# Paged attention on one core: projections of two token tiles by seven block products, with stored weight sums and head columns passed through DRAM

## The chip, the core and the metric

The kernel runs on one core of one Trainium2 chip. The metric is the device time of one launch in microseconds (us). The kernel before took 2164.35 us, the median of three runs between 2163.95 and 2166.38. Its profile is one further execution with a span of 2166.3 us.

Engine names are those of the profile: PE is the matmul engine (PEld its weight loads), DVE the vector engine, ACT the scalar engine, POOL GpSimd, and SP the engine whose queue issues most DMA transfers.

## The reference

There are 64 sequences of 32 tokens with 512 channels. All arithmetic is in fp32.

```
x = x + einsum('bct,bcd->bdt', x, weights[condition])      # a 32x32 mix of tokens per sequence
q, k, v = x Wq^T, x Wk^T, x Wv^T                           # 32, 8 and 8 heads of 128
q, k = rope(rmsnorm(q) * q_norm_w), rope(rmsnorm(k) * k_norm_w)
keys, values = 512 cached positions by page table, then the 32 new ones
x = x + softmax(q keys^T / sqrt(128), masked by cache length) values Wo^T
```

Four query heads share one key head. The page table of a sequence names 16 pages of 32 positions.

## The kernel before

Tokens are packed into 16 tiles of 128 rows, four sequences to a tile. The heads are worked in two halves of 16 query heads and 4 key heads, so there are 32 **steps**: 16 tiles for half 0 and then the same tiles for half 1. Half 0 keeps the transposed input and the running output of a tile in DRAM (`x1t_d`, `acc_d`) and half 1 loads them again.

A step has 16 **slots**: four sequences (batches) by four key heads. In each slot PE does the `scores` of one head (four 128x128 products) and, one slot later, its `values` (four 128x129 products). Into these slots the loop at L949 lays other work by a table (`pieces`, L888): while step n runs its attention, step n+1 gets its projections. `k_a` stands at slot 3, the four `q_a` at slots 4 to 7 and `v_a` at slot 13; each is four 128x512 products (`project`, L420). The output projection of step n-1 stands at slots 8 and 9 with eight 128x512 products each (`out_proj`). At slot 0 `new_scores` (L606) reads all the head columns of the step, and at slots 1 and 3 `new_values` follows.

A projected group goes through `norm_rope` (L428): a square on ACT, a power on POOL and about seven operations on DVE. `turn_rows` then transposes 32x32 blocks into the SBUF tile `rows`, and `spread` (L482) copies them by DMA, sixteen transfers a step, to the tiles `q_cols` and `q_last` in which heads lie as columns. `spread` of three batches stands at slot 9, that of batch 2 at slot 11, since `q_cols` of a batch is free only when its scores have been done.

Cached keys come by `load_k` (L292): sixteen page transfers of 64 KB for each batch, issued by SP two batches ahead, into two buffers. `head_keys` (L582) copies one head of them on DVE into one of four `kh` buffers, four slots before the scores read it. Cached values are gathered by POOL, one 256 KB chunk a slot, and masked by ACT.

PE and SP work in the order in which the program is written (`manual_schedule`). On DVE, ACT and POOL a scheduler set the order when the kernel was built. An engine that meets a wait holds everything behind it. The SP queue is therefore one line for key pages, spreads, inputs and stores. A last part of the code (`exact`) repeats the whole computation with masks and is entered only where a denominator leaves its range.

Of the kernel before, what the change touches and what calls it, by code (L numbers as in the profile page):

```python
# [19 lines left out]
P = 128  # L20
# [28 lines left out]
RAW = 3  # L49
WARM = 10  # L50
# [5 lines left out]
def cond_resid_paged_attention_kernel(  # L56
# [52 lines left out]
    bd = const.tile([P, P], F32, tag="bd", name="bd")  # L109
    nc.vector.memset(bd, 0.0)  # L110
# [8 lines left out]
    cos = const.tile([P, NT, HD], F32, tag="cos", name="cos")  # L119
    sin = const.tile([P, NT, HD], F32, tag="sin", name="sin")  # L120
# [10 lines left out]

    def angles(t0, tmp):

        reduced(t0, tmp)
        sines(t0, tmp)
# [19 lines left out]
    def sines(t0, tmp):  # L155
        t1 = t0 + TRIG
        _, turns, red = (tmp[:, i, :] for i in range(3))
        nc.scalar.activation(sin[:, t0:t1, :].rearrange("p t f -> p (t f)"), red, AF.Sin)
        nc.scalar.activation(turns, red, AF.Abs)
        nc.scalar.activation(  # L160
            cos[:, t0:t1, :].rearrange("p t f -> p (t f)"),
            turns,
            AF.Sin,
            bias=half_pi,
            scale=-1.0,
        )
# [21 lines left out]
    acc_d = [dram.tile([P, HID], F32, tag=f"acc_d{t}", name=f"acc_d{t}") for t in range(NT)]  # L188

# [5 lines left out]
    def steps_of(exact, pools):  # L195
# [34 lines left out]
        rows = wpool.tile([P, 4, GH + 1, P], F32, tag="rows", name=f"rows_{uid}")  # L230
# [48 lines left out]
        def load_cond_weights(t, eng=nc.sync, kind=mybir.EngineType.SP):  # L279
            number = conditions(t, kind)  # L280
            for i in range(BT):
                blk = slice(i * S, (i + 1) * S)
                eng.dma_start(
                    bd[blk, blk],
# [69 lines left out]
        class Step:  # L354
            def __init__(self, n):
                self.n, self.hh, self.t = n, n // NT, n % NT
                self.name = f"{n}_{uid}"

        def x1_a(st):

            st.acc = work.tile([P, HID], F32, tag="acc", name=f"acc_{st.name}", bufs=3)
# [9 lines left out]
        def x1_c(st):  # L371
# [3 lines left out]
            nc.tensor.matmul(pm, bd, st.acc, start=True, stop=True)  # L375
            nc.vector.tensor_tensor(st.acc, pm, st.acc, ALU.add)

        def x1_b(st):
# [5 lines left out]
            st.x1t = work.tile([P, KC, P], F32, tag="x1t", name=f"x1t_{st.name}", bufs=1)  # L384
# [7 lines left out]
        def rot_tables(st):  # L392

            st.rot = {}
            c, s = cos[:, st.t, :], sin[:, st.t, :]
            for name, w in norm_w.items():
                cw = work.tile(
                    [P, 2, HD],
                    F32,
                    tag=f"cw_{name}",  # L400
                    name=f"cw_{name}_{st.name}",
                    bufs=1,
                )
                sw = work.tile(
                    [P, 2, HD],
                    F32,
                    tag=f"sw_{name}",
                    name=f"sw_{name}_{st.name}",
                    bufs=1,
                )  # L410
                w1, w2 = w[:, 0:HD], w[:, HD:D]
                nc.gpsimd.tensor_tensor(cw[:, 0, :], w1, c, ALU.mult)
                nc.gpsimd.tensor_tensor(cw[:, 1, :], w2, c, ALU.mult)
                nc.vector.scalar_tensor_tensor(
                    sw[:, 0, :], w2, -1.0, s, ALU.mult, ALU.mult
                )
                nc.gpsimd.tensor_tensor(sw[:, 1, :], w1, s, ALU.mult)
                st.rot[name] = cw, sw
# [9 lines left out]
        def norm_rope(st, pp, name, kind, to=None):  # L428

            cw, sw = st.rot[kind]  # L430
# [39 lines left out]
        def turn_rows(st, i, rd, name):  # L470


            nc.vector.transpose(
                rows[:, :, i, :].rearrange("p k (h s) -> p h k s", h=4),
                rd.rearrange("p h (k d) -> p h k d", k=4),
            )

        def columns(st, bt):

            return q_last[st.n % 2] if bt == BT - 1 else q_cols[:, bt]  # L480

        def spread(st, batches):  # L482


            for bt in batches:
                for k in range(4):
                    nc.sync.dma_start(
                        columns(st, bt)[k * S : (k + 1) * S, :, :],
                        rows[bt * S : (bt + 1) * S, k, :, :],
                    )  # L490
# [3 lines left out]

# [610 lines left out]
```

## Time and profile before

| What | Value |
|---|---|
| Median of three runs | 2164.35 us |
| Profiled execution, span | 2166.3 us |
| PE busy | 2144.2 us, 99% of the span |
| DVE busy | 1196.5 us, 55% |
| ACT busy | 868.9 us, 40% |
| POOL busy | 804.7 us, 37% |
| 128x512 products in q, k and v projections | 768, shown as 1536 instructions |
| DMA moved | 357.51 MB, mean 165 GB/s |
| SP transfers of key pages | 2048, 64 KB each |
| SP transfers of head columns | 480, 80 KB each |

An fp32 product is two matmul instructions in the profile, so a projection of four products is a line with x8. Matmuls overlap, so a product is priced by the distance from start to start, and not by its busy time. A DMA that SP issues is shown with the time that SP needs for the issue; the transfer itself goes on after it.

### The profile page before, as it was taken

What the parts mean: (1) busy time and instruction counts of PE and PEld (TensorE: products, weight loads), DVE (VectorE), ACT (ScalarE), POOL (GpSimd) and SP (SyncE); (2) the same over time, 40 slices, a digit from 0 to 9 for tenths busy, and PEclk for the clock granted to TensorE, in tenths of its full rate; (3) what the DMA queues carried; (4) which work ended last, traced back from release to release, by engine and by line L of the source; (5) the groups of instructions that cost most, each with busy time, mean ns of one, the idle gap of its engine ahead of it and who ended that gap; (6) DMA issues with size and microseconds to landing.
All of it is one profiled execution on the core that took longest, in us unless ns stands there. A gap on an engine that the chain in (4) does not pass through costs nothing.

```text
span 2166.3 us, 41552 instructions
## 1 busy us (share of the span) xinstructions
PE 2144.2 (99%) x12972; PEld 1494.4 (69%) x12972; DVE 1196.5 (55%) x2883; ACT 868.9 (40%) x1577; POOL 804.7 (37%) x1005
## 2 busy tenths in 40 slices
PE   7999999999999999999999999999999999999998
PEld 4766777667776677766777766777666777667775
DVE  5666555666455564465554565644566545556442
ACT  3544444444333344333444333443334443334441
POOL 4433333433333343333433343433434333334330
PEclk9999999999999999999999999999999999999999
DMA  8765555555655556556766855565545565555551
GB/s 248 193 164 162 157 172 157 148 155 160 172 152 152 151 160 174 154 150 196 224 177 179 212 158 164 157 178 159 156 141 169 162 174 159 153 153 163 171 162 54
DMA packets 387638, 357.51 MB, mean 165 GB/s; under 512 B 55024, under 2 KB 317296, under 8 KB 387408
## 3 DMA queue, kind: packets, MB, share of 16 engines
q1 hardware_dynamic: 342864, 213.87, 35.1%
q0 software_dynamic: 41648, 136.74, 21.6%
q10 hardware_dynamic: 2896, 4.14, 0.5%
q8 instruction: 106, 1.74, 0.3%
q14 instruction: 124, 1.02, 0.2%
HBM read 302.64 MB, written 12.58 MB: 146 GB/s over the span
## 4 chain that ended last, share of the span: by engine, by line
PE 97%; ACT 0%; issue 0%; DVE 0%
PE po_x L653 22%; PE ps_x L595 21%; PE pout_x L541 20%; PE pp_q_x L423 20%; PE pp_k_x L423 5%; PE pp_v_x L423 5%; PE pnv_x L637 2%; PE psn_x L613 1%; PE pmix_x L375 1%; PE px1t_x L383 0%; PE pt_x L467 0%; ACT pr_x L603 0%; ACT v_x L346 0%; DVE acc_x L549 0%; ACT nv_x L645 0%
## 5 line engine op out<-in xcount | busy, mean ns | idle before, releaser
L333 POOL DMA_INDIRECT raw_x<-in_vc_dram,v_row x512 | 540.4, 1055 | 820.4 <-ACT v_x L346 752.0
L603 ACT ACTIVATE pr_x<-ps_x 128x512 f32<-128x512 f32 x512 | 305.9, 597 | 825.5 <-PE ps_x L595 756.8
L653 PEld LDWEIGHTS po_x<-v_x,pr_x 128*128 128x128 f32 x4096 | 515.7, 192 | 126.9 <-issue 114.5
L653 PE MATMUL po_x<-v_x,pr_x 128*128 128x129 f32 x4096 | 551.1, 277 | 2.3 <-ACT pr_x L603 1.6
L423 PE MATMUL pp_q_x<-wq_x,x1t_x 128*128 128x512 f32 x1024 | 463.2, 595 | 8.5 <-ACT x1t_x L385 8.2
L541 PE MATMUL pout_x<-wo_x,ot_x 128*128 128x512 f32 x1024 | 450.2, 592 | 0.0
L595 PE MATMUL ps_x<-q_cols_x,kh_x 128*128 128x128 f32 x3072 | 405.4, 275 | 0.0
L595 PEld LDWEIGHTS ps_x<-q_cols_x,kh_x 128*128 128x128 f32 x3072 | 376.1, 192 | 15.1 <-issue 14.6
L346 ACT ACTIVATE v_x<-raw_x,valid 128x512 f32<-128x512 f32 x512 | 363.0, 716 | 5.3 <-DMA raw_x<-in_vc_dram,v_row 5.1
L541 PEld LDWEIGHTS pout_x<-wo_x,ot_x 128*128 128x128 f32 x1024 | 189.7, 190 | 214.3 <-issue 214.0
L423 PEld LDWEIGHTS pp_q_x<-wq_x,x1t_x 128*128 128x128 f32 x1024 | 185.8, 191 | 194.4 <-issue 185.6
L588 DVE COPY kh_x<-k_t_x 128x512 f32<-128x512 f32 x506 | 206.0, 417 | 188.1 <-PE ps_x L595 153.8
L671 DVE TENSOR_TENSOR nv_x<-po_x,nv_x 128x258 f32<-128x258 f32 x256 | 108.4, 424 | 314.9 <-PE po_x L653 279.9
L440 POOL TENSOR_TENSOR rs_q_x<-ms_q_x,minus_half 128x4 f32<-128x4 f32 x128 | 140.8, 1100 | 170.1 <-DVE ms_q_x L438 169.9
L433 ACT ACTIVATE sq_q_x<-pp_q_x 128x512 f32<-128x512 f32 x128 | 76.6, 598 | 272.9 <-PE pp_q_x L423 178.9
L595 PE MATMUL ps_x<-q_last_x,kh_x 128*128 128x128 f32 x1024 | 135.2, 275 | 0.0
L549 DVE TENSOR_TENSOR acc_x<-pout_x,acc_x 128x512 f32<-128x512 f32 x32 | 22.1, 692 | 199.3 <-PE pout_x L541 199.3
L595 PEld LDWEIGHTS ps_x<-q_last_x,kh_x 128*128 128x128 f32 x1024 | 124.6, 192 | 0.0
L423 PE MATMUL pp_k_x<-wk_x,x1t_x 128*128 128x512 f32 x256 | 116.3, 597 | 0.9 <-ACT x1t_x L385 0.9
L423 PE MATMUL pp_v_x<-wv_x,x1t_x 128*128 128x512 f32 x256 | 115.2, 592 | 0.0
L674 DVE TENSOR_TENSOR o_x<-nv_x,rden 128x256 f32<-128x256 f32 x256 | 108.6, 424 | 6.2
L437 DVE TENSOR_REDUCE ms_q_x<-sq_q_x 128x4 f32<-128x512 f32 x128 | 86.5, 676 | 45.1 <-ACT sq_q_x L433 44.6
(105 smaller groups left out, 1455.1 us busy)
## 6 DMA issues: line engine op xcount, KB each, us to landing
k_t_x<-in_kt_dram SPq DMA_DIRECT2D x2048, 64.0 KB
q_cols_x<-rows_x SPq DMA_DIRECT2D x360, 80.0 KB
q_last_x<-rows_x SPq DMA_DIRECT2D x120, 80.0 KB
raw_x<-in_vc_dram,v_row POOLq DMA_INDIRECT x512
wo_x<-in_wo_dram SPq DMA_DIRECT2D x32, 256.0 KB
acc_x<-in_x_dram SPq DMA_DIRECT2D x16, 256.0 KB
acc_d<-acc_x SPq DMA_DIRECT2D x16, 256.0 KB
wq_x<-in_wq_dram SPq DMA_DIRECT2D x8, 512.0 KB
```

The lines of the kernel that those rows point to most:

```text
L333: nc.gpsimd.indirect_dma_start(out=raw.rearrange("p g d -> p (g d)"), out_offset=None, in_=vc, in_offset=bass.IndirectOffsetOnAxis(ap=v_ro ...
L346: nc.scalar.activation(v_bufs[b % 2][:, c, :, 0:D], raw, AF.Copy, scale=ok)
L423: nc.tensor.matmul(pp, st.x1t[:, c, :], w[:, c, :], start=(c == 0), stop=(c == KC - 1))
L437: nc.vector.tensor_reduce(ms, sq, AX.X, ALU.add)
L440: nc.gpsimd.tensor_tensor(rs, ms, minus_half, ALU.pow)
L541: nc.tensor.matmul(st.po, st.ot[:, i, :], wt["o", st.hh, i // 4][:, i % 4, :], start=(i == 0), stop=(i == QH - 1),)
L588: last["dve"] = nc.vector.tensor_copy(k, ba.k_raw[:, :, g, :]).ins
L595: nc.tensor.matmul(ps[:, c, :], ba.k[g][:, c * P : (c + 1) * P], queries(ba, g), start=True, stop=True,)
L603: last["act"] = nc.scalar.activation(pr, ps, AF.Exp, scale=SCALE).ins
L653: nc.tensor.matmul(ba.po[:, g % 2, :], ba.pr[g][:, c, :], ba.v_t[:, c, g, :], start=(c == 0), stop=(c == VC - 1),)
L671: nc.vector.tensor_tensor(t, ba.po, t, ALU.add)
L674: nc.vector.tensor_tensor(ba.o[:, both, :], t[:, :, 0:D], rd.unsqueeze(2).to_broadcast([P, 2, D]), ALU.mult,)
```

## The change

From tile 4 on, in both halves, the projections of two neighbouring tiles (steps 2m and 2m+1) are made together by a `Pair`. The two tiles and the two halves of the 512 channels make a 2x2 block matrix of inputs; two weight groups and the two channel halves make a 2x2 block matrix of weights. Their product takes seven block products where it took eight, each of two 128x512 matmuls. Three such sets (q0 with q1, q2 with q3, k with v) replace the twelve projections of two steps. Tiles 0 to 3 of half 0 are projected as before.

- **Input sums.** `sums_x` makes four sums of input blocks on DVE for each pair.
- **Weight sums.** For the first pair of each half DVE makes four sums of weight blocks for each set (`sums_w`, `sums_w4`). One replaces its weight in place, three are stored to DRAM (`sums_d`). Each later pair loads these three for each set, 512 KB each, into two buffers (`load_sums`).
- **Sets.** A set is spread over four slots: `p1_p6` (four matmuls), `p5_p2` (four), `p7` (two) and `p4_p3` (four). In the even step before the pair (n = 2m-2) set 0 stands at slots 4, 5, 6 and 8 and set 1 at 10, 11, 12 and 14. Set 2 stands at slots 4, 5, 6 and 8 of the odd step n+1. Five additions on DVE and one copy on ACT combine the products of a set. `norm_rope` then reads its input from SBUF in three of four cases.
- **Head columns.** A turned group is stored to DRAM (`heads_d`) by SP two slots later, and `spread` reads from there. For the first tile of a pair the spreads stand at slots 13 and 14 of the odd step, for the second at slots 10 and 12 of the even step.
- **Room in SBUF.** The tables of sines and cosines are stored and loaded for each tile (`rot_d`), the residual is stored early and loaded again (`keep_x1`, `reload`). `kh` has three buffers for four, so `head_keys` runs three slots ahead, and `pr` has two for three.

```diff
+KH = 3
+KEEP = 2
+        def turn_rows(st, i, rd):
+            part = work.tile([P, 4, P], F32, tag="slab", name=f"rows{i}_{st.name}", bufs=SLABS)
+            nc.vector.transpose(...)
+            kept.append(
+                lambda: nc.sync.dma_start(
+                    heads_d[st.n][i], part.rearrange("p k c -> p (k c)")
+                )
+            )
         def spread(st, batches):
+            src = heads_d[st.n].rearrange("i (b d) (k c) -> b k d i c", b=BT, k=4)
             for bt in batches:
                 for k in range(4):
-                    nc.sync.dma_start(
-                        columns(st, bt)[k * S : (k + 1) * S, :, :],
-                        rows[bt * S : (bt + 1) * S, k, :, :],
-                    )
+                    nc.sync.dma_start(columns(st, bt)[k * S : (k + 1) * S, :, :], src[bt, k])
+        def load_sums(pair, k, i):
+            t = sums_tile(f"t{i + 2}_{pair.name}_{k}")
+            nc.sync.dma_start(t, sums_d[pair.hh][k][:, i, :])
+            pair.t[k, i] = t
+            def p1_p6():
+                t[2], t[3] = made[pair.hh, k] if first else (pair.t[k, 0], pair.t[k, 1])
+                b11, t["b21"], t[1], t["b22"] = halves(pair.hh, k)
+                t["a"], t["b"] = bank("pa"), bank("pb")
+                product(t["a"], A11, b11, True)
+                t["z"] = temp("z")
+                nc.scalar.copy(t["z"], t["a"])
+                product(t["b"], S2, t[2], True)
+                t["u2"] = temp("u2")
+                add(t["u2"], t["b"], t["z"])
+                ...
+            def p5_p2():
+                t["c"] = bank("pc")
+                product(t["c"], S1, t[1], True)
+                product(t["a"], A12, t["b21"])
+                done(s0, e0, t["a"])
+            def p7():
+                product(t["b"], S3, t[3])
+                ...
+            def p4_p3():
+                ...
+                product(t["b"], A22, t[4])
+                add(t["z"], t["b"], t["z"])
+                product(t["c"], S4, t["b22"])
+                ...
+                done(s1, e0, t["z"])
+                if e1[0] != "v":
+                    done(s0, e1, t["u2"])
         def head_keys(ba, g, eng=None):
-            k = work.tile([P, NPP, PSIZE], F32, tag="kh", name=f"kh_{ba.name}_{g}", bufs=4)
+            k = spare.get(("kh", ba.n, g))
+            if k is None:
+                k = work.tile([P, L], F32, tag="kh", name=f"kh_{ba.name}_{g}", bufs=KH)
...
+        for pair in pairs:
+            s0, s1 = pair.both
+            n = s0.n - 2
...
+                where = [
+                    (0, n, (4, 5, 6, 8)),
+                    (1, n, (10, 11, 12, 14)),
+                    (2, n + 1, (4, 5, 6, 8)),
+                ]
+            for k, m, slots in where:
+                fresh = early or half_first
+                set_of(pair, k, m, slots, fresh)
+                if fresh:
+                    at(m, slots[0] - 2, lambda pair=pair, k=k: sums_w(pair.hh, k))
+                else:
+                    at(m, slots[0] - 2, lambda pair=pair, k=k: load_sums(pair, k, 0))
+                    at(m, slots[0] - 1, lambda pair=pair, k=k: load_sums(pair, k, 1))
+                    at(m, slots[0], lambda pair=pair, k=k: load_sums(pair, k, 2))
+            spread_of(s0, 13, 14)
+            spread_of(s1, 10, 12)
...
-                    if later is not None:
-                        head_keys(later, g)
+                    while copied <= min(this.n * GH + g + KH, NHH * NT * BT * GH - 1):
+                        head_keys(this if copied // GH == this.n else later, copied % GH)
+                        copied += 1
```

## The prediction

> **What bounds the kernel now.** I read the page's busy times first, then its chain.
>
> ```profile
> PE 2144.2 (99%) x12972; PEld 1494.4 (69%) x12972; DVE 1196.5 (55%) x2883; ACT 868.9 (40%) x1577; POOL 804.7 (37%) x1005
> ...
> PE 97%; ACT 0%; issue 0%; DVE 0%
> ```
>
> PE is busy for 99% and is 97% of the chain, so PE work taken away shortens the end by its own length, as long as nobody keeps PE waiting. The price of PE work comes from the chain in order of time, here from slot 11 of step 20 to slot 0 of step 21 (start, length, what).
>
> ```profile
> 1425.09 0.89 PE po_x L653 x8
> 1425.99 0.89 PE ps_x L595 x8
> ...
> 1428.67 3.44 PE pp_v_x L423 x8
> ...
> 1436.57 0.89 PE ps_x L595 x8
> 1437.46 1.01 PE psn_x L613 x32
> ```
>
> A slot with scores and values alone lasts 0.89 + 0.89 = 1.79 us. Four 128x512 products last 3.44 us, 0.859 each. The slots of a step are very uneven: with half an output projection, eight products, 8.66 us.
>
> Next I read the timeline of SP, because the change puts nearly all its new transfers there (start, length, line).
>
> ```profile
> 1425.12 2.41 SPq L487 DMA_DIRECT2D q_cols_x<-rows_x  x4
> 1427.63 0.53 SPq L363 DMA_DIRECT2D acc_x<-acc_d  x1
> 1429.56 4.84 SPq L306 DMA_DIRECT2D k_t_x<-in_kt_dram  x8
> ...
> 1435.07 39.96 SPq L306 DMA_DIRECT2D k_t_x<-in_kt_dram  x52
> ```
>
> SP issues slowly and almost without rest: eight key pages take 4.84 us. Sixteen take about 9.2 us, 0.57 each. The last spread of the next step is issued before these pages, 11 us before `psn` needs it, and the trace's packets show its last bytes at 1429.90, 2.4 us after SP's last issue. The price of 32-partition pieces loaded from DRAM stands in an earlier stretch of the same view, 0.49 us each:
>
> ```profile
> 65.70 2.97 SPq L257 DMA_DIRECT2D wo_x<-in_wo_dram  x6
> ```
>
> The waits of SP name its gate (us in total, times, longest): pages wait for the DVE copy that frees their buffer.
>
> ```profile
> SPq L306 <- DVE kh_x L588: 195.1, 33, 8.3
> ```
>
> DVE's timeline prices its operations: where work is dense a 128x512 operation starts 0.60 us after the one before, though each is listed with 0.69.
>
> ```profile
> 1466.15 0.68 DVE L444 TENSOR_TENSOR rope_q_x<-pp_q_x,cw_q_x 128x512 f32<-128x512 f32 x1
> 1466.75 0.16 DVE L438 TENSOR_SCALAR ms_q_x<-ms_q_x 128x4 f32<-128x4 f32 x1
> ```
>
> Last, the start shows what an idle PE costs: PE's timeline and two windows, whose last three columns are the granted clock, the DMA share and GB/s.
>
> ```profile
> 16.96 6.05 PE L423 MATMUL pp_q_x<-wq_x,x1t_x 128*128 128x512 f32 x8 [8.23 <-ACT x1t_x L385]
> ...
> 14.00:18.00 4.00, 1.04 (x2) 0.52 (x3) 2.12 (x11) 1.38 (x4) 1.48 (x6) 0.50 1.05 377
> 18.00:22.00 4.00, 4.00 (x7) 1.65 (x6) 3.21 (x16) 0.00 (x0) 0.24 (x1) 0.53 0.54 156
> ```
>
> After 8.23 us without work the clock was 0.50. From its start to that of the next group this one took 5.89 us where 3.44 is usual, 2.4 lost.
>
> [...]
>
> **Removed.** Fourteen pairs make 42 products where they made 48: 14 x 6 = 84 products x 0.859 = **-72.2 us** of PE.
>
> **Added on DVE.** Five additions a set, fifteen a pair, at 0.60 are 9.0 us for each two steps, and four sums of inputs at 0.34 are 1.4. The work that hides them is the attention on PE: a pair of steps needs 126 us of it. But the even step now holds eight of the pair's ten `norm_rope`, about 3.8 us each from the same timeline, so set 1 keeps DVE busy into the next step. Behind it waits the third key copy ahead (`kh_0_3`), which frees the key buffer of SP. With p5_p2 ending 9.6 us after slot 10 starts, I count the built order from there at 0.60 for a 128x512 operation, 0.34 for a copy or a half-size operation: `kh_0_3` is done 28.8 us after slot 10, which is 6.0 after slot 0 of the odd step. In the weight sums of the first pair of each half, three 128x1024 additions a set at about 1.2 (twice 0.60) are in the same queue; I give them 1 us of delay a pair. ACT exchanges its two copies of v for three copies a pair, some 0.6 us more, hidden in its 60% of idle time. The SBUF reads of `norm_rope` I price like its PSUM reads (from -0.1 to +0.1 us each, hidden except in the count above).
>
> **Moved on SP: the spread of a pair's first tile.** It stands at slots 13 and 14 of the odd step. In the built order SP then has: eight pages (slot 12), twelve spread copies, eight pages, four spread copies. The gate of the first page is a copy of `kh`, which with three buffers must wait for the scores of slot 12 itself (before: slot 11, and the spread stood ahead of it). From the start of slot 12:
>
> - scores 0.9, copy and signals 0.6: 1.5
> - 8 pages x 0.57: 4.6
> - 12 copies x 0.48: 5.8 (pieces of 512 B from DRAM are not in the trace in this form; ends: 0.43 as a 256 KB load nearby, 0.63 as the copies from `rows` had; I take the nearest row, `wo`)
> - 8 pages: 4.6; 4 copies: 1.9; landing: 2.4
>
> The sum is 20.8 us. PE needs the last column in `new_scores`, four bare slots and one set of scores later: 4 x 1.79 + 0.9 = 8.1. It waits **12.7 us**. That is so in nine odd steps (13 to 29). In steps 5 to 11 PE also mixes and transposes the next inputs (2.5 us) and SP loads one more input (0.6): 10.8. In step 3 `p4_p3` at slot 12 covers another 3.4: 7.4. Sum 9 x 12.7 + 4 x 10.8 + 7.4 = **165 us**. Each such wait is long enough for the slow clock: 14 x 2.4 = **34 us**. With 0.43 or 0.63 for a copy the sum is 154 or 198. The next products, the exponentials and the output of the step all stand behind `new_scores` on PE. The second tile's spread lands about 2 us ahead of its use, since its step has three more pieces of a set after slot 11.
>
> **Added on SP: weight sums.** For set 2, SP must issue 16 pages (9.2), two stores of heads (0.8), in half 1 two tables (0.8) and the first sum (0.45) after `kh_0_3`, and 512 KB land some 3.5 us later (2.4 for small ones, and twice the bytes of any transfer there). So the sum is there 6.0 + 14.8 = 20.8 us after slot 0. The second product of `p1_p6` wants it at 3.0 + 2.7 + 1.8 + 2.7 + 0.9 + 1.7 = 12.8 after (slots 0 to 3, scores, first product). Taking half a microsecond off for pages issued without a hiccup, PE waits **7.5 us** in half 1 and 6.6 in half 0: 7 x 7.5 + 5 x 6.6 = **85 us** in the twelve pairs that load, and 12 x 2.4 = **29 us** of slow clock. The unknown is the landing of 512 KB: 2.4 to 6 us, so 72 to 116. Sums of set 0 and 1 come about 1 us ahead of use: long slots (8 and 9) or the wait above lie before them. The stores of heads (0.4 each), residuals and tables fit in SP's gaps of the long slots: SP is asked for about 109 us of 126 a pair. If that cover is gone, they add 0.4 each to the second wait.
>
> **Sum.** 2166.3 - 72.2 + 165 + 34 + 85 + 29 + 2 = 2409; I take five off for waits that overlap: **2404 us**. The profiled execution lies 2 us over the median, which is less than the rounding here.
>
> **Rivals.**
>
> - *The queue keeps up* (faster): 2166 - 72 = 2094, or up to 2160. PE's 99% speaks for it, and so does a DMA share of mostly five or six tenths. It decides at a price: if one of the 32 transfers after the gate cost at most 0.13 us, nothing would wait; at 0.29 the first wait would eat the gain alone. Measured are 0.48 and 0.57. 0.05.
> - *Only the spread is late*: `kh_0_3` and the weight sums come in time since DVE runs ahead. 2166 - 72 + 165 + 34 = 2293. For it speaks that the second wait rests on a long count of DVE. 0.18.
> - *DMA saturates too*: some 8 MB more a pair (2.6 stored heads, 4.7 sums, the rest residuals and tables) slow the pages and value rows, each 1 us on a page's batch or gather. PE waits in the bare slots as well: eight batches x 14 pairs x 1 us over the forecast, 2515. Against it: the mean was 165 GB/s, and windows at the start moved 377. 0.13.
>
> **How the numbers follow.** Forecast 0.62, the rivals as given, 0.02 for anything near 2164. The forecast's own span is 2330 to 2480 (copies 0.43 to 0.63, landings, half the slow clock). Adding the case with one wait gives **2280 to 2485**. A measurement of this kernel can tell 0.2% from no change. Faster 0.05, same 0.01, slower 0.94.
>
> **What would show it.** Right: the chain holds SP or DMA with 10% or more; `psn` and `ps` on PE wait for `q_cols<-heads_d` some 9 to 13 us in fourteen places, the set-2 products for `t<-sums_d` about 7 us in twelve; the granted clock drops after each; PE does 84 products (168 instructions) of 128x512 fewer. Wrong: SP issues these transfers faster than 0.3 us, the first page of slot 12 goes out before that slot's scores, or the PE gaps lie in the bare slots instead.

## The result and the profile after

The changed kernel takes 2575.53 us, the median of four runs from 2565.65 to 2576.18, against 2164.23 us for the kernel before beside it. The ratio is 1.189, with an interval of 1.187 to 1.191. The prediction was 2404 us in a range of 2280 to 2485: the direction and the two waits were right, the size was not.

The profiled execution took 2563.9 us. Of its page, first the busy times, then the chain that ended last.

```profile
PE 2223.6 (87%) x12804; PEld 1562.0 (61%) x12804; DVE 1368.3 (53%) x3142; ACT 870.2 (34%) x1593; POOL 797.3 (31%) x911
...
PE 53%; DMA 15%; SPq 13%; DVE 11%; issue 5%; ACT 1%; POOL 0%; DVEq 0%; ACTq 0%; POOLq 0%
```

PE has 168 instructions fewer (12804 for 12972), the 84 products that were to go. But its busy time rose by 79 us instead of falling by 72, and its share of the chain fell from 97% to 53%. SP and DMA now hold 28% of the chain. The list of waits (us in total, times, longest) says where PE stands still.

```profile
PE psn_x L822 <- DMA q_cols_x<-heads_d: 109.3, 17, 9.1
PE pb_x L662 <- DMA t_x<-sums_d: 77.4, 19, 9.0
PE ps_x L801 <- DMA q_cols_x<-heads_d: 47.4, 9, 7.9
PE pmix_x L392 <- DMA acc_x<-in_x_dram: 17.5, 4, 7.2
PE pnv_x L846 <- ACT nv_x L854: 17.5, 13, 2.9
PE pmix_x L392 <- DMA q_cols_x<-heads_d: 17.2, 3, 6.1
PE pb_x L662 <- DVE t L642: 15.2, 3, 6.2
```

The first, third and second rows are the two waits of the prediction: 156.7 us for columns and 77.4 for weight sums. The other four are 67.4 us that it did not have, but for 2 us of fresh sums. In the sixth the profile names the columns, which `pmix` does not read. In e1 below, where the columns come earlier, `pmix` waits in the same three places (21.1 us, put down to key pages), so I count this row as late inputs too.

The first wait can be followed in the second half, from slot 12 of step 21 on. PE's timeline (start, length, line, in brackets the wait before it):

```profile
1793.91 1.06 PE L801 MATMUL ps_x<-q_last_x,kh_x 128*128 128x128 f32 x8
...
1805.78 2.04 PE L801 MATMUL ps_x<-q_cols_x,kh_x 128*128 128x128 f32 x8 [4.56 <-DMA q_cols_x<-heads_d]
...
1815.24 0.60 PE L822 MATMUL psn_x<-q_cols_x 128*32 128x128 f32 x2 [6.67 <-DMA q_cols_x<-heads_d]
```

and SP's timeline of the same stretch:

```profile
1795.46 4.03 SPq L321 DMA_DIRECT2D k_t_x<-in_kt_dram  x8
1799.53 4.20 SPq L526 DMA_DIRECT2D q_cols_x<-heads_d  x8
1803.78 2.38 SPq L526 DMA_DIRECT2D q_last_x<-heads_d  x4
1806.35 5.13 SPq L321 DMA_DIRECT2D k_t_x<-in_kt_dram  x8
1811.59 1.86 SPq L526 DMA_DIRECT2D q_cols_x<-heads_d  x4
```

Eight pages, twelve copies, eight pages, four copies, in that order. What stands behind a page that waits goes out after it: SP's waits ahead of pages for `kh_x` are 214.2 us in all, 65 times, 13.2 at most. The first page goes out 1.55 us after slot 12 starts (1.5 in the prediction), and `psn` goes on 21.3 us after it (20.8 in the prediction). Within this stretch PE waits twice, for the first columns and for those of batch 2, with 2.8 us of work between.

What that does to the clock shows in the windows of the same place and of a place in step 21 (busy us of the engines; the last three columns are granted clock, DMA share, GB/s):

```profile
1805.00:1809.00 4.00, 2.79 (x12) 2.14 (x12) 0.43 (x1) 1.08 (x2) 0.00 (x0) 0.50 1.05 214
...
1815.00:1821.00 6.00, 5.76 (x48) 5.20 (x51) 1.04 (x4) 0.60 (x1) 0.21 (x1) 0.53 0.38 108
1821.00:1825.00 4.00, 4.00 (x47) 3.88 (x48) 1.87 (x4) 2.99 (x7) 0.00 (x0) 1.00 0.34 94
...
1742.00:1749.00 7.00, 7.00 (x33) 5.74 (x32) 2.59 (x7) 5.21 (x12) 2.37 (x3) 0.51 0.66 193
```

From 1804 to 1821 PE runs at half clock. The trace's record of the granted clock has 50 such stretches in the execution, 407 us in all, where the kernel before had two. One in the opening and one after the last product are in both kernels, so 48 are new. PE's busy time gives an estimate of their price: 2223.6 - (2144.2 - 72.2) = 151.6 us.

So the profiled time is: 2166.3 - 72.2 + 301.5 (the seven rows of waits) + 151.6 (clock) = 2547, and 17 us of smaller waits. The term of the clock is what is left of the busy time, so this sum closes by construction.

### The profile page after: what moved, and what is told of

Same layout as the page of the kernel before. It is cut to its first block, busy times and chain, and to the rows that moved or that the text cites. A ratio compares the mean times of both kernels' runs of the same rounds, so it can differ in the third digit from the quotient of the medians.

```text
span 2563.9 us, 42379 instructions
## 1 busy us (share of the span) xinstructions
PE 2223.6 (87%) x12804; PEld 1562.0 (61%) x12804; DVE 1368.3 (53%) x3142; ACT 870.2 (34%) x1593; POOL 797.3 (31%) x911
## 2 busy tenths in 40 slices
DMA packets 501885, 478.69 MB, mean 187 GB/s; under 512 B 60912, under 2 KB 407920, under 8 KB 501648
## 4 chain that ended last, share of the span: by engine, by line
PE 53%; DMA 15%; SPq 13%; DVE 11%; issue 5%; ACT 1%; POOL 0%; DVEq 0%; ACTq 0%; POOLq 0%
PE pout_x L740 13%; PE po_x L862 11%; PE ps_x L801 10%; SPq L321 10%; PE pb_x L662 7%; DMA q_cols_x<-heads_d 5%; DMA t_x<-sums_d 4%; PE pc_x L662 4%; PE pa_x L662 4%; DMA k_t_x<-in_kt_dram 3%; DVE ropeu_q_x L482 2%; SPq L526 1%; DVE kh_x L794 1%; DVE ms_q_x L468 1%; PE psn_x L822 1%
## 5 line engine op out<-in xcount | busy, mean ns | idle before, releaser
L862 PEld LDWEIGHTS po_x<-v_x,pr_x 128*128 128x128 f32 x4088 | 547.7, 202 | 136.7 <-issue 124.2
L862 PE MATMUL po_x<-v_x,pr_x 128*128 128x129 f32 x4088 | 584.2, 288 | 0.9 <-ACT v_x L361 0.8
L801 PE MATMUL ps_x<-q_cols_x,kh_x 128*128 128x128 f32 x3064 | 426.3, 284 | 53.9 <-DMA q_cols_x<-heads_d 47.4
L801 PEld LDWEIGHTS ps_x<-q_cols_x,kh_x 128*128 128x128 f32 x3064 | 394.4, 201 | 58.1 <-issue 56.8
L662 PE MATMUL pb_x<-t_x,x_x 128*128 128x512 f32 x432 | 225.9, 649 | 81.4 <-DMA t_x<-sums_d 77.4
L678 DVE TENSOR_TENSOR u_x<-pb_x,z_x 128x512 f32<-128x512 f32 x84 | 58.1, 692 | 234.9 <-PE pb_x L662 194.8
L662 PEld LDWEIGHTS pb_x<-t_x,x_x 128*128 128x128 f32 x432 | 80.5, 205 | 163.8 <-issue 153.5
L822 PE MATMUL psn_x<-q_cols_x 128*32 128x128 f32 x768 | 59.9, 342 | 109.5 <-DMA q_cols_x<-heads_d 109.3
L364 POOL COPY v_x<-valid 128x16 f32<-128x16 f32 x128 | 32.5, 254 | 357.8 <-PE po_x L862 357.2
L822 PEld LDWEIGHTS psn_x<-q_cols_x 128*32 128x32 f32 x768 | 38.8, 133 | 122.0 <-issue 66.8
```

What stands on the lines that cost most here:

```text
L662: nc.tensor.matmul(bank, pair.x[:, i, c, :], w[:, c * 512 : (c + 1) * 512], start=start and c == 0, stop=c == 1, skip_group_check=not start,)
L801: nc.tensor.matmul(ps[:, c, :], ba.k[g][:, c * P : (c + 1) * P], queries(ba, g), start=True, stop=True,)
L822: nc.tensor.matmul(ps[own, g, :], columns(st, bt)[:, GH, g * S : (g + 1) * S], columns(st, bt)[:, g, :], start=True, stop=True,)
L862: nc.tensor.matmul(ba.po[:, g % 2, :], ba.pr[g][:, c, :], ba.v_t[:, c, g, :], start=(c == 0), stop=(c == VC - 1),)
```

## The experiments

Times are medians, with the ratio to the kernel before that ran beside it.

| Kernel | us | ratio, interval |
|---|---|---|
| after | 2575.5 | 1.189 (1.187 to 1.191) |
| e1: first tile's spread early | 2508.9 | 1.159 (1.157 to 1.161) |
| e2: weight sums by ACT | 2463.7 | 1.137 (1.134 to 1.140) |
| e3: both | 2354.7 | 1.089 (1.087 to 1.092) |
| e4: idle time of PE filled | 2556.0 | 1.182 (1.180 to 1.184) |
| e6: eight products again | 2655.2 | 1.228 (1.225 to 1.230) |
| e7: before, 14 spreads late | 2338.1 | 1.080 (1.078 to 1.082) |
| e8: SP left with pages and spreads | 2237.6 | 1.034 (1.031 to 1.038) |
| e10: e8, first tile's spread late | 2429.1 | 1.123 (1.121 to 1.125) |
| e11, e12: e8 mended; with heads on SP | 2209.7; 2258.1 | 1.020 (1.018 to 1.022); 1.042 (1.040 to 1.044) |
| e13, e14: mended further; spreads by ACT | 2185.9; 2240.5 | 1.009 (1.006 to 1.012); 1.032 (1.029 to 1.035) |
| e15, e16: after and e1 with heads by ACT | 2578.7; 2508.1 | 1.191 (1.189 to 1.193); 1.158 (1.155 to 1.160) |
| e17, e18, e19: e13 with loads by POOL | 2178.6; 2174.8; 2179.2 | 1.009 (1.005 to 1.012); 1.004 (1.003 to 1.006); 1.005 (1.003 to 1.006) |

### The two waits, one at a time and together

```diff
-            spread_of(s0, 13, 14)
+            spread_of(s0, *((13, 14) if early else (9, 11)))     # e1, e3
-            nc.sync.dma_start(t, sums_d[pair.hh][k][:, i, :])
+            nc.scalar.dma_start(t, sums_d[pair.hh][k][:, i, :])  # e2, e3
```

> The changed kernel with one edit: the spread of a pair's first tile stands at slots 9 and 11 of the odd step, ahead of the gated key pages, in all pairs but the first (which has its keys too late for that). Theory A (two separate waits, each with a stretch of slow clock behind it): the waits of psn, ps and pmix for q_cols<-heads_d go, some 170 us of idle PE, and with them roughly half of the 150 us that the slow clock costs, so 2576 - 170 - 75 = about 2330 us (2290 to 2370), while the waits of pb for t<-sums_d stay near 80 us. Rival B (SP's queue as a whole is too slow, and a transfer moved forward makes another late): the waits for weight sums or keys grow by what the spread gives, 2480 to 2576.

> The changed kernel with two edits: the spread of the pair's first tile at slots 9 and 11 (not in the first pair), and the loads of the weight sums issued by ACT's queue instead of SP's. The same bytes move. Theory A (both waits come from what stands ahead of them in SP's queue): some 290 of the 320 us of gaps and most of the 150 us of slow clock go, so about 2140 us (2100 to 2190). Rival B (the DMA engines or the landing of 512 KB are the limit, not the order in the queue): products still wait for t<-sums_d some 5 us each, 2250 to 2400. Rival C (the blocked loads on ACT hold up the exponentials): values on PE wait for pr, also over 2250.

> The changed kernel with one edit: the loads of the weight sums are issued by ACT's queue instead of SP's; the spread stays at slots 13 and 14. With the early spread this edit was worth 154 us (2509 to 2355), since there the second product of set 0 waited too. Theory A (one queue, several late transfers, and a wait hides those that come after it: in the changed kernel set 0's sums are late behind the wait of psn): the waits for t<-sums_d go, about 80 us of idle time and some 25 us of slow clock, 2455 to 2490 us. Rival B (the waits are independent and add): 2576 - 154 = 2422 us, within 15.

The early spread gained 67 us, where theory A wanted 240. The waits of PE in e1:

```profile
PE pb_x L662 <- DMA t_x<-sums_d: 168.7, 28, 10.1
PE psn_x L822 <- DMA q_cols_x<-heads_d: 34.7, 5, 8.3
```

The wait for columns is gone but for five places, and that for weight sums has doubled. In e1 the second product of set 0, in slot 4 of every even step from 18 to 28, waits some 8.7 us; in the changed kernel it doesn't wait there. PE's timeline in e1 and, below the dots, of the same product of step 20 in the changed kernel:

```profile
1788.47 3.75 PE L662 MATMUL pb_x<-t_x,x_x 128*128 128x512 f32 x4 [8.77 <-DMA t_x<-sums_d]
...
1672.86 1.88 PE L662 MATMUL pb_x<-t_x,x_x 128*128 128x512 f32 x4
```

Set 0's sums had been late all along, behind a wait that ended later. So rival B took e1.

With both edits the time fell by 221 us, not 435. The time lies in the range of rival B, but not for its reason: the loaded weight sums no longer appear among PE's waits at all, nor does `pr`, which rival C named. In their place stands a third transfer:

```profile
PE pmix_x L392 <- DMA acc_x<-in_x_dram: 62.4, 10, 9.8
PE psn_x L822 <- DMA q_cols_x<-heads_d: 62.1, 17, 8.9
```

SP's timeline of e3 in step 11 shows why the inputs of the next tiles are late:

```profile
948.28 3.81 SPq L526 DMA_DIRECT2D q_cols_x<-heads_d  x8
...
954.04 0.43 SPq L380 DMA_DIRECT2D acc_x<-in_x_dram  x1
...
960.22 8.24 SPq L321 DMA_DIRECT2D k_t_x<-in_kt_dram  x8
968.51 0.43 SPq L380 DMA_DIRECT2D acc_x<-in_x_dram  x1
```

Each input stands behind a block of other transfers, and `pmix` waits for it, 8.3 us before slot 12 and 5.4 before slot 14. e2 settled how the parts add: 112 us for the sums alone, inside theory A's range and outside rival B's. 67 and 112 are 179, together they give 221: each wait hides part of the next.

### The first wait by itself

```diff
 # e7, on the kernel before: pieces of the tiles 4, 6, 8 ... 30
-                9: ((spread, (0, 1, 3)),),
-                11: ((spread, (2,)),),
-                13: (v_a,),
+                **(
+                    {13: ((spread, (0, 1, 3)), v_a), 14: ((spread, (2,)),)}
+                    if st.n > 3 and st.n % 2 == 0
+                    else {9: ((spread, (0, 1, 3)),), 11: ((spread, (2,)),), 13: (v_a,)}
+                ),
```

> The kernel before with one edit: in the 14 odd steps that feed the first tile of a later pair (3, 5 and so on to 29) the spread stands at slots 13 and 14, where the change puts it, instead of 9 and 11; everything else, four key buffers and copies from SBUF too, is as before. Theory A (the place in SP's queue alone makes psn wait): from the start of slot 12, 8 pages x 0.57, 12 copies x 0.60, 8 pages, 4 copies and 2.4 to land are 20.9 us; PE needs the columns after 8.1 and v's 3.4, in the first half after another 2.5 of mixing; 7 x 9.4 + 7 x 6.9 = 114 us of wait and 30 to 70 of slow clock, 2310 to 2350 us. Rival B (with four key buffers the gate of the pages opens a slot earlier and SP has the time): 2165 to 2230 us.

The result lies in theory A's range. The row of PE's waits in e7:

```profile
PE psn_x L613 <- DMA q_cols_x<-rows_x: 136.9, 17, 10.5
```

That kernel has four key buffers, the old copies and no weight sums; the place in SP's queue alone makes the wait. PE's busy time is 2180.0, 35.8 more than before. That is **2.6 us for each of 14 waits** (2.4 in the prediction), and the record of the clock has 14 new stretches at half clock.

The same edit the other way round, on a kernel in which SP has nothing else:

```diff
 # e8: keep_x1, keep_rot, load_rot, load_x, load_sums, heads, stores, reload,
 #     x1_a from step 2 on, load_cond_weights: nc.sync -> nc.scalar
-            spread_of(s0, 13, 14)
-            spread_of(s1, 10, 12)
+            spread_of(s0, *((13, 14) if early else (9, 11)))     # e10: 13, 14
+            spread_of(s1, 10, 11)
```

> The changed kernel with SP kept for key pages, spreads and o's weights: from step 2 on, the inputs and their mixing weights, residuals, rope tables, stored heads, stored and loaded weight sums, inputs of pairs and output stores are issued by ACT; the spread of a pair's first tile stands at slots 9 and 11 (not in the first pair), that of the second at 10 and 11. The same bytes move. Theory A (the order in SP's queue is the cause of nearly all of the loss): what is left of it is in the first pairs of a half, 2094 to 2160 us. Rival B (ACT's own waits ahead of its transfers hold up exponentials and copies of values): PE waits for pr or v, over 2200 us. Rival C (the DMA engines can't carry the extra 53 MB in time): PE waits for q_cols or kh in bare slots, 2200 to 2330 us.

> As the run with everything but pages, spreads and o's weights on ACT, but the spread of a pair's first tile stands at slots 13 and 14 again: the first wait alone, with the queue otherwise free. Theory A (21.3 us from the start of slot 12 to psn, of which 8.1 are work: 13 us of wait in 14 places and the slow clock behind it, 3 to 5 us each): 14 x 13 + 14 x 4 = about 240 us more than that run. Rival B (with a free queue the pages' gate is no longer late, and the wait is short): 0 to 100 us more.

e10 takes 192 us more than e8. The first pair keeps its slots in both, so that is 14.7 for each of 13 places. The prediction's first wait with its slow clock, less that of step 3, was 189; this run's theory A wanted 240. In e1 the same edit had been worth 67. e8 itself stays 78 us above the top of theory A's range, in that of B and C, but not for their reasons alone. (Rival C's 53 MB are near the loaded weight sums; in all the changed kernel moves 121 MB more than the kernel before.) Some of PE's waits there:

```profile
PE ps_x L801 <- DVE kh_x L794: 32.8, 24, 7.7
...
PE psn_x L822 <- DMA q_cols_x<-heads_d: 30.4, 5, 10.7
...
PE pout_x L740 <- DMA wo_x<-in_wo_dram: 12.9, 1, 12.9
...
PE po_x L862 <- ACT pr_x L812: 9.8, 7, 2.7
```

The first row is key copies on DVE. The second is late columns in steps 4, 14, 18 and 31, the third late weights in step 17, the last what B had in mind.

### The slow clock by itself

```diff
+        def hold(to, n):                       # e4
+            for _ in range(n):
+                nc.tensor.matmul(to, ident, ident, start=True, stop=True)
...
+            if ba.st.n > NT and ba.st.n % 2 == 0 and ba.bt == g == 0:
+                hold(ps[:, 0, :], 16)
...
             ps = ps_p.tile([P, GH, P], F32, tag="pp", name=f"psn_{st.name}")
+            if st.n > 3 and st.n % 2 == 0:
+                hold(ps[:, 0, :], 22 if st.n > NT else 28)
...
+                if k == 2 and not first:
+                    hold(t["b"][:, 0:P], 14 if pair.hh else 28)
                 product(t["b"], S2, t[2], True)
```

> The changed kernel with idle time filled: 128x128 products of two constants, into PSUM that the next product overwrites, stand in PE's queue just ahead of the products that wait (16 of them ahead of the first scores of an even step in the second half, 22 or 28 ahead of psn, 14 or 28 ahead of the second product of set 2), 0.22 us each at full clock, a little less than the waits last. Nothing else moves. Theory A (the slow clock behind the waits costs time of its own, about 150 us, where the prediction had 63): the clock stays at 1.0 behind most waits and the time falls by 90 to 150 us, to 2425 to 2485. Rival B (SP's transfers set the times, and PE's slowness only fills what would be longer waiting): the waits grow by what the clock gives, and the time stays within 20 us of 2576. Rival C (the fillers cost what they last): 2650 and more.

The mean granted clock rose from 0.921 to 0.963 and the time fell by 20 us only: rival B. From PE's records: the fillers were busy for 157.6 us of 2330.7, so PE's own work took 2173.1, 50.5 less than in the changed kernel. Its waits and the fillers together make 366.0, against 329.2 of waits in the changed kernel: the waits grew by 36.8. Three quarters of what the clock gave went back into waiting, as if the transfers that PE waits for came no sooner. The fillers left 36 slow stretches, so this tells the direction, not the whole price.

### The saved work put back

```diff
                 product(t["c"], S1, t[1], True)
+                product(t["c"], S1, t[1], True)        # e6
```

> The changed kernel with the saved work put back: the block product of p5 is issued twice in every set, so a pair has 48 products of 128x512 again, 84 more at 0.859 us. Theory A (the seven-for-eight saving is real and adds to the waits, since the extra products stand ahead of what opens SP's gates): 72 us more, 2630 to 2650. Rival B (the saving was swallowed by the waits, which shrink when PE has more to do): 0 to 30 us more, 2576 to 2606.

The time rose by 80 us, 5 over theory A's range. The saving of seven for eight is real, and it was not swallowed by the waits. In the profiles PE's busy time rose by 57.8 us and its idle time by 26; that the extra products stand ahead of the gates is the likely reason that the waits did not shrink in return.

### Are the stores of heads a cause?

```diff
             kept.append(
-                lambda: nc.sync.dma_start(
+                lambda: nc.scalar.dma_start(           # e15, e16 (with the early spread)
                     heads_d[st.n][i], part.rearrange("p k c -> p (k c)")
```

In the changed kernel SP waits long ahead of these stores:

```profile
SPq L515 <- DVE nv_x L880: 131.3, 26, 8.1
SPq L515 <- DVE rows_x L510: 28.5, 16, 5.3
```

> The changed kernel with one edit: the stores of heads are issued by ACT instead of SP. The prediction took 0.4 us of SP for each; in the profile of the changed kernel SP waits 131.3 + 28.5 us for DVE ahead of them, with key pages queued behind. Theory A (that wait is part of what the prediction lacks): 40 to 100 us less, 2475 to 2535 us. Rival B (SP waits there while nothing behind it is due): 0 to 20 us less, 2555 to 2580 us.

> The changed kernel with the spread of a pair's first tile at slots 9 and 11 (alone 2509 us) and the stores of heads on ACT. Theory A (the stores' wait for DVE makes the weight sums and inputs late that are queued behind it): 2400 to 2460 us. Rival B (the weight sums are late for their own place, behind the pages): 2490 to 2515 us.

Both differences are within the spread of the runs (+3 and -1 us). So SP waits there while nothing behind it is due, or what is due is late for another reason; which of the two is not shown. The long wait of the queue was no cost here.

### Mending the queues

```diff
 # e11, from e8
-            at(weights[0], weights[1], lambda: load_cond_weights(st.t, nc.scalar, mybir.EngineType.Activation))
+            at(weights[0], weights[1], lambda: load_cond_weights(st.t, nc.gpsimd, mybir.EngineType.Pool))
-            spread_of(s0, *((13, 14) if early else (9, 11)))
+            spread_of(s0, *((12, 13) if early else (9, 11)))
-                        load_parts(outputs, 1, part)
+                        load_parts(outputs, 1, part, nc.scalar)     # q, k and v of half 1 too
+                            nc.scalar if st.n > 3 and (slot > 13, slot < 2)[st.n % 2] else None,   # head_keys
 # e12, from e11: heads_d by nc.sync
 # e13, from e11
-                        load_parts(outputs, 1, part, nc.scalar)
+                        load_parts(outputs, 1, part, nc.gpsimd)
-            spread_of(s1, 10, 11)
+            spread_of(s1, 8, 11)
+                            nc.scalar if st.n > 3 and st.n % 2 == 0 and slot == 15 else None,
...
 # e14, from e13: spread by nc.scalar      e17, from e13: load_sums by nc.gpsimd
 # e18, from e17: heads_d by nc.gpsimd     e19, from e18: x1_a, store, reload by nc.gpsimd
```

> The kernel with all but pages and spreads off SP, further mended where its steps are still longer than their work on PE: the second half's weights loaded by ACT's queue (step 17 waited 12.9 us for o's weights on SP, step 14 9.5 for columns behind q's), mixing weights loaded by POOL's queue instead of ACT's, the first pair's spread at slots 12 and 13 ahead of all pages of that batch (15.3 us of wait in step 4), the second tile's tables kept by SP, and the key copies of slots 14 and 15 of an even and 0 and 1 of an odd step made by ACT (DVE is 1.7 us late with one in every odd step). Theory A (what is left are single late transfers and copies, each removable): 75 to 100 us less than 2238, 2135 to 2165 us, so at or below the 2165 of the kernel before. Rival B (each mend makes another transfer or copy late): 2190 to 2240 us.

> As the run before it, but the ten stores of heads of a pair are issued by SP again, as in the changed kernel, so ACT never waits for DVE's transposes ahead of an exponential. Theory A (a store of 0.4 us on SP that waits for DVE blocks the key pages behind it, in the half step where DVE is late): 10 to 40 us more than that run. Rival B (these stores are rarely late, and ACT gains more than SP loses): 0 to 20 us less.

> As the mended kernel at 2210 us, with its own remaining waits taken on: the second half's weights go by POOL's queue (on ACT they held up exponentials: step 17 ran 12.6 us over its work on PE, step 13 10.1, step 15 7.5), ACT makes only the key copy of slot 15 of an even step (four copies made pnv wait 1.1 to 1.7 us in each odd step), rope tables, kept inputs and inputs of pairs return to SP, the second tile's spread stands at slots 8 and 11, and the first pair's last two sets and its spread stand a slot earlier (11 us of wait in step 4, 5.3 in step 31). Theory A (each of these waits has its own cause, as named): 35 to 60 us less, 2150 to 2175 us. Rival B (the room on SP and ACT is used up, so that a transfer put back makes pages or columns late): 2200 to 2240 us.

> As the mended kernel at 2186 us, but the sixteen copies of a spread are issued by ACT too (twelve of them in slot 8 or 9, where PE is busy for 8.66 us with half an output projection), so SP has key pages and a few small loads only. In the run before it SP issued from 1509 to 1640 us almost without a pause, 64 pages in 49.2 us (0.77 each), and PE waited for key copies that waited for pages. Theory A (what bounds the mended kernel is SP's rate: a pair's 128 pages at 0.77 and 32 copies at 0.45 are 113 us of its 131): 32 x 0.45 = 14 us a pair come free, the waits of ps for kh go, 15 to 40 us less, 2145 to 2170 us, at or below the kernel before. Rival B (ACT's issuing holds up the exponentials as much): 2180 to 2210 us.

e11 gained 28 us where 75 to 100 were expected. PE's longest waits there are for ACT (`pnv` for `nv`, 24.3 us, 19 times), which had taken on weights and key copies in one run, so the two are not told apart. In e12, heads on SP cost 48 us, a little over theory A's 10 to 40; the same move was worth nothing in the changed kernel. e13, in which tables, kept inputs and inputs of pairs also went back to SP and the first pair's last sets stood a slot earlier, gained 24 more, under theory A's 35 to 60. In e14 ACT paid for what SP was spared, rival B and more: 55 us slower. Waits of ACT and PE there:

```profile
ACT pr_x L812 <- DMA k_t_x<-in_kt_dram: 129.7, 25, 14.8
ACT pr_x L812 <- DMA q_cols_x<-heads_d: 61.0, 8, 13.5
...
PE po_x L862 <- ACT pr_x L812: 21.3, 17, 5.4
```

In e13 a wait of SP stood out that the data do not explain, since a key page needs no weight sum:

```profile
SPq L321 <- DMA t_x<-sums_d: 102.5, 44, 6.6
SPq L321 <- DVE kh_x L794: 76.0, 27, 11.7
```

> The mended kernel at 2186 us with the loads of the weight sums issued by POOL instead of ACT. In that kernel's profile SP waits 102.5 us, 44 times, for t_x<-sums_d before a key page, though a page needs nothing of it. Theory A (a load of 512 KB that ACT issues takes one of the places for transfers under way that SP's next page needs; POOL's transfers have others): these waits go and the time falls by 15 to 40 us, 2145 to 2170 us. Rival B (the DMA engines are shared, and SP waits for something else instead): 2175 to 2200 us.

> As the run before it, and the stores of heads on POOL too (SP waits 55.4 us for heads_d<-rows_x before a page in the mended kernel). Theory A (as there): up to 20 us less than that run. Rival B (POOL, waiting for DVE's transposes, is late with the powers of the norms that DVE needs next): 20 us or more longer than that run.

> As the mended kernel at 2175 us, with the inputs, residuals and output stores on POOL as well, so that ACT issues nothing after the opening but the stores of fresh weight sums, and the last spread of the second tile a slot earlier. In that kernel SP still waits some 80 us for residuals, outputs and inputs of ACT's queue before a page or a spread. Theory A (these are places among the transfers under way that ACT's loads take): 5 to 20 us less, 2155 to 2170 us, level with the kernel before. Rival B (what is left is DVE, late with key copies in each odd step, and the gates of the pages): 2170 to 2180 us.

With the sums issued by POOL this row is gone from SP's waits, but SP's wait ahead of pages for another of ACT's transfers, `heads_d<-rows_x`, is 118.7 us, and the median fell by 7 us only, less than its runs scatter (2169.6 to 2192.5): rival B. e18 is 4 us below it, within that scatter; its rival B, which wanted 20 more, is out. e19 stays there (rival B).

What such a wait is can be read from the semaphores in the records of the traces: each transfer names the one that it carries, and the record of landings logs the updates (57658 in the changed kernel). In these programs the transfers of SP and of ACT take turns on the same eight semaphores (numbers 100 to 107; 3083 transfers of SP and 21 of ACT in the changed kernel), those of POOL on eight others (109 to 116; 519 transfers). Most transfers of SP (2602 of 3083 in the changed kernel, 2372 of 2651 in e13) wait, before they are issued, for the very semaphore that they carry, so for an earlier transfer that carried it, and that can be one of ACT's. Theory A of e17 was right on this point, though not on its worth in time. By the same records such waits of SP last 43 us in all in the kernel before, 147 in the changed kernel, 246 in e3, 384 in e13 and 214 in e18. Moving loads to ACT frees SP's line, but not these places. No run gave ACT semaphores of its own.

The page of e18 and its longest wait of PE:

```profile
PE 2108.5 (97%) x12804; PEld 1486.9 (68%) x12804; DVE 1346.3 (62%) x3128; ACT 873.3 (40%) x1605; POOL 1012.3 (47%) x1249
...
PE ps_x L801 <- DVE kh_x L794: 27.4, 26, 3.6
```

PE is busy for 97% again. No version beat the kernel before; e18 is 0.4% above it.

## Why the prediction was wrong, step by step

Two terms failed. The slow clock was priced for 26 stretches, 63 us, and there were 48, 151.6 us. The waits for inputs, for `pnv` and for fresh sums were put at 2 us and came to 67.4. The two large waits came out near their sums, the second in part by luck.

For each step of the program the trace gives its length and PE's instructions. Priced at the start-to-start distances of the kernel before, a pair of steps needs 127.2 us of PE in the second half and 129.2 in the first. What a pair lasts beyond that, as a mean over steps 20 to 27 and 6 to 13:

| us a pair | second half | first half |
|---|---|---|
| predicted (two waits, two slow stretches) | 25.0 | 22.2 |
| after | 28.9 | 33.6 |
| e1 | 26.5 | 26.6 |
| e2 | 19.5 | 24.3 |
| e3 | 5.5 | 17.8 |
| e10 | 19.1 | 23.7 |
| e8 | 3.4 | 6.2 |
| e18 | 2.2 | 6.1 |

- **Removed, 72 us.** Right: 168 instructions fewer, and having the products back costs 80 us in e6.
- **First wait, 165 us.** Right in its place, its order of transfers and its size: 156.7 us in two rows, 192 with its slow clock by e10 against e8 (189 predicted for these 13 places). In the stretch shown the sum is 21.3 us for 20.8, but its parts cancel: the first eight pages take 4.1 us (4.6), the twelve copies 6.8 (5.8). PE waits 11.2 us of it (12.7), since its own work there takes 10.1 (8.1), partly at half clock.
- **Weight sums, 85 us.** The row says 77.4; taken away in e2 they give 9.4 and 9.3 us a pair, where 9.9 and 9.0 were predicted, and 112 us in all (114). The 108 issues themselves cost SP 0.42 us each, 46 us; the rest is the wait in line, and the slow clock behind it. The size is partly luck. In the second half the waits of set 2 are 3.5 to 7.3 us, for 7.5: the sums arrive later than predicted, 22.6 to 25.0 us after slot 0 begins for 20.8, but PE too comes late to them, by a pause of `pnv` and a slow stretch. In the first half they are 5.6 to 9.0, for 6.6.
- **"Sums of set 0 and 1 come about 1 us ahead of use: long slots or the wait above lie before them."** For set 0 it was the wait above. In e1 these sums are 8.7 us late. The step did little to the time of the changed kernel, but it would have misled anyone who mended the first wait by it.
- **"SP loads one more input (0.6)" in steps 5 to 11, taken as cover.** This step failed. The input is itself late: `pmix` waits 21.6 us in these steps and 13.1 in steps 1 to 3, and in the first half a pair takes 33.6 us where 22.2 were predicted. Part of it takes the place of the first wait: `psn` waits 7.4 to 8.2 us in these steps, for 10.8. e3 shows that input as the next transfer due once the two waits are gone; in e8, where inputs do not pass through SP, the first half falls from 17.8 to 6.2. e8 moves other transfers too, so the inputs' own share of that is argued from the row of `pmix`.
- **Slow clock, "14 x 2.4" and "12 x 2.4", 63 us.** The price of one stretch was right (2.6 in e7). That each wait would be long enough was an estimate from one pause, the 8.23 us of the opening; in the changed kernel each of the 45 pauses of PE that last 3.5 to 9.1 us is followed by such a stretch or lies in one. The count was not right: 48 new stretches for 26, at 3.2 us, 151.6 in all. The first wait comes in two pieces, inputs add a third, and seven more follow pauses of 1.84 us of `pnv`.
- **The stores of heads "fit in SP's gaps".** Right for the changed kernel (e15, e16), though SP waits 160 us ahead of them.
- **The count of DVE.** Right for its purpose in the second half: SP's pages wait for the key copy until 6.5 to 6.7 us after slot 0 of the odd step begins (6.0 predicted), and the first sum goes out at 16.9 to 18.1 (16.8 by the prediction's terms). In step 23, whose slot 0 begins at 1887.54, SP's timeline has:

```profile
1894.05 8.20 SPq L321 DMA_DIRECT2D k_t_x<-in_kt_dram  x16
...
1904.87 0.87 SPq L649 DMA_DIRECT2D t_x<-sums_d  x2
```

In steps 5 to 11 the pages wait until 8.8 to 9.8. `norm_rope` reads from SBUF at about the price of its PSUM reads, as assumed: 0.68 us for both on DVE, 0.63 for 0.60 on ACT. What the count left out is `nv`: in step 21 ACT's copy of it waits 5.47 us for DVE's `o_x`, and behind that copy `pnv` on PE pauses 1.84 us.

In the sum of the profile: the waits of `pmix`, `pnv` and fresh sums are 65 us more than predicted, the slow clock 89, smaller waits 17, the overlap that I took off 5; the two waits are 16 less. That is 160, the distance from 2404 to 2563.9. By place, before the five taken off, steps 4 to 13 are some 60 us over the predicted pairs of the table, steps 16 to 29 some 34, and steps 0 to 3, 14, 15, 30 and 31 the other 61.

This is a list of terms, not of causes that could be taken away one by one. e4 shows that the part of the slow clock's term that was removed mostly turned into waiting, and e1 that a wait removed uncovers the next. Of the rivals, the queue that keeps up and the spread as the only late transfer fall with the rows of waits. The rival that DMA saturates is out too: e18 moves 478.71 MB, as the changed kernel does (478.69), in 2175 us.

What stays open: e18's 0.4%. Its pairs last 2.2 and 6.1 us longer than PE's work, with PE waiting for key copies of DVE. That DVE has more to do (1196.5 us before, 1346.3 there) is a likely reason, and so are the shared semaphores; no run took work off DVE or gave ACT other semaphores.

## What to carry to other kernels

When several transfers stand in one issuing queue, work out the lateness of every one behind the gate, also of those that a longer wait now hides: mending the first wait alone was worth 67 us, with the queue free it was worth 192. Price a wait on PE with its slow stretch (2.6 us here for a wait of some 10), and count its pieces, but don't add the two as if each could be won alone. Before saving 3% of the bounding engine's work, ask what the change asks of the queues that feed it: here 72 us of products were saved for 121 MB more of transfers (357.51 to 478.69), and no order of them that I tried came out ahead.

## What was not expected of the hardware

- **A short pause can be followed by half clock.** In the seven odd steps from 17 to 29 PE pauses 1.84 us ahead of `pnv`. Each time a stretch at half clock follows, four times of 6.8 us and three times of 3.4, during which PE works on without such a pause (the window from 1742 to 1749 above). The prediction counted on waits of 6.6 us and more, and in the opening of the kernel before the half clock starts 2.8 us after the last product, in a pause of 8.23 us; here less is enough. Length alone does not decide: pauses of 1.77 and 2.12 us ahead of `pb` (at 872 and 1035) were followed by none, nor was one of 1.60 us late in the last step of the kernel before.
- **A second issuing queue was not a separate one.** SP waited for ACT's transfers through the semaphores that the two share (384 us of waits for its own transfers' semaphores in e13). That is how these programs were built; the runs don't show it to be a rule of the chip.
